# Moving a residual stage beside a recurrence, and reordering the maxima of an attention loop

## The chip, the cores and the metric

The kernel runs on one core of one Trainium2 chip. The metric is the device time of one execution in microseconds (us); the time of a kernel is the median of several runs. The engines are named as in the profile: PE is TensorE (PEld its weight loads), DVE is VectorE, ACT is ScalarE, POOL is GpSimd, SP is SyncE, which here only issues DMAs.

## The reference

The input `x` has 2 batches of 2048 positions with 256 features. A recurrent layer comes first, then mixture-of-experts attention, each with a layer norm ahead and a residual behind:

```python
x = x + rnn(layernorm(x), Wi, bi, Wh, bh)       # h = tanh(Wi x_t + bi + Wh h + bh)
x = x + ffn(layernorm(x), Wq, Wk, Ws, Wd, Wv, Wo)
# ffn: 8 heads of 64, 5 experts, 2 of them chosen
q = (x @ Wq).reshape(b, t, h, dh).transpose(0, 2, 1, 3)
k = (x @ Wk).reshape(b, t, h, dh).transpose(0, 2, 1, 3)
gl_v = (x @ Ws).reshape(b, t, h, e)
wv = _topk_mask(gl_v, SEL) * jax.nn.sigmoid(gl_v)
xv = jnp.einsum('btd,edk->btek', x, Wv)
v = jnp.einsum('bthe,btek->bhtk', wv, xv)
scores = jnp.einsum('bhid,bhjd->bhij', q * scale, k)
probs = jax.nn.softmax(scores, axis=-1)
attn = jnp.einsum('bhij,bhjd->bihd', probs, v)
mask_o = _topk_mask((x @ Wd).reshape(b, t, h, e), SEL)
out = jnp.einsum('bthe,bthk,ekd->btd', mask_o, attn, Wo)
```

Everything is float32.

## The kernel before, in words

**Layout.** Position `n * 16 + s` belongs to segment `n` (128 of them, on the partitions) and to chunk `s` (16 of them). A chunk is thus one step of all 128 segments, and the recurrence over 2048 positions is run on 128 segments side by side.

**Preparation** (L219 to L246). Groups of 1, 1, 2, 4, 4, 4 chunks: statistics on DVE (`stats`, L122 and L123), an inverse root from a bit trick (`guess`, L129 to L135) and four Newton steps of three tiny DVE operations each (`newton`, L142 to L146); normalisation on POOL (L156), four PE transposes (L231), a copy on ACT (L235), the input projection on PE, and ACT adds the sum of the two biases (`bsum`) on the way to `xi` (L246).

**Recurrence** (L261 to L294). `run("a")` starts every segment from zero and takes 16 steps; its last states become the start states `ends` of the segments behind. `run("b")` takes the 16 steps again from these and keeps every state in `hs`. A step is 16 weight loads and products (L283), four additions on DVE (L290) and four tanh on ACT (L293). Then DVE compares the last states of the two runs (L300 to L305), PE sums the verdict over the partitions (`pc`, L307), DVE makes it a flag (`again`, L309), and every engine loads it and branches (L310, L311). If the states still differ, the run is repeated under the branch; with these inputs it isn't.

**Residual stage** (L319 to L384), in two halves of 8 chunks. PE turns the states back (`tpb`, L334), DVE adds them to `x` (L335), SP stores the sum (`x1d`), DVE makes statistics and scales of batch 0. POOL and DVE normalise one chunk of each pair, PE turns it (`tpc`, L349), ACT copies it to `xn2T` (L352); PE makes the gate logits (`pg`, L359), ACT copies them to `gates_all` (L367). For each of the 16 chunks PE makes the experts' values (`pxv`, L372), ACT or DVE copies them (L381, L383) and SP stores them (`xvd`, L384). Batch 1 does this later, inside attention (`load_late` to `logits_late`).

**Attention** (from L497). A unit is one (batch, head) and one block of 512 queries; there are 64. A unit has 8 tiles of scores, `c` = 0 to 7, each for 256 keys (128x1024); a step `T` makes two, so four steps make a unit, and the boundary step is `T % 4 == 0`. The life of a tile:

- `scores`: PE writes it to one of two PSUM buffers (`s`, L503); `stage`: ACT copies it to SBUF (`p`, L514); `largest`: DVE takes the running elementwise maximum (`m`, L525; in the last tile `mh`, `m`, `mm`, L528 to L531). Tile 0 has no `m`; the `m` of tile 1 reads the copy of tile 0.
- In the next unit's boundary step PE turns the maximum (`pm`, L538), DVE reduces it (`mq`, L543), and PE spreads it over the partitions (`pt`, L553), which ACT copies to `top` (L556).
- From five steps behind on, `subtract` takes the maximum from the tile (L563; DVE for tiles 0 and 1, POOL for the rest), `exponential` is on ACT (L566), `products` on PE (`o`, L576), `fold` adds tiles in pairs with a DMA issued from POOL's queue (L588), `sums` makes the denominators on PE (`d`, L597).
- The closing of a unit: `take`, `take_sums` (`os`, L612 to L620), `close`: PE turns it (`po`, L629), DVE makes `den`, its reciprocal, `mr` and `pro` (L631 to L642), and `gather` adds it to memory (L684).

Keys (`pk`), queries (`pq`), the experts of batch 1 (`pv`, L463) and the value mixes (`fetch`, `xq`, `v`) of a head are made inside the loop. `gates` ranks the experts of half the chunks (`choose`, L160 to L195: ACT copies the logits and a ramp, DVE compares, POOL counts). Everything small in PSUM (`pm`, `pt`, `po`, `pk`, `pq`, `pv`, `py`, `pz`, `mh`, `wp`) comes from one pool of two buffers, `misc`.

**What sets the order.** Up to attention a scheduler orders each engine's instructions. Attention is in an order written out by hand, and each engine does its queue in it. A step lists: `take`; the subtraction of tile 0 where the step is the one in which a unit's subtractions begin (`T % 4 == 1`); one exponential; for each new tile scores, stage, largest; the subtractions and the fold; the list `before` of this step; products and sums; the other exponential; the list `behind` of this step. The lists are filled ahead by `at(table, T, f, ...)`:

```python
for t in new:
    ss = scores(t)
    stage(t, ss)
    largest(t, ss)
...
    at(before, T1, turn_max, u)
    at(before, T1, reduce_max, u)
    at(behind, T1, spread_max, u)
```

Since `close` of an earlier unit comes into the list `behind` of the same boundary step ahead of `spread_max`, PE has `po` before `pt`. Where two engines read the same scores in PSUM, one waits for the other: `m` of a tile waits for its copy.

Of the kernel before, what the change touches and what calls it, by code (L numbers as in the profile page):

```python
# [14 lines left out]
P = 128  # L15
# [5 lines left out]
def rnn_then_switchhead_kernel(  # L21
# [60 lines left out]
    nc.vector.tensor_tensor(bsum, bias[:, 0, :], bias[:, 1, :], ALU.add)  # L82
# [67 lines left out]
    def scales(pool, mv, n, nm):  # L150

        neg, v, y = guess(pool, mv, n, nm)
        return neg, newton(pool, v, y, n, range(4), nm)
# [6 lines left out]
    def choose(pool, b, c0, n, half, nm, logits):  # L160
# [8 lines left out]
        nc.scalar.copy(  # L169
# [3 lines left out]
        if not half:  # L173
            sg = pool.tile([P, n, HE], F32, tag="sg", bufs=1, name=f"sg{nm}")
            nc.scalar.activation(sg, gl, AF.Tanh, scale=0.5)
        later = []
        for d in range(1, E):
            a = pool.tile([P, n, H, E - d], F32, tag=f"later{d}", bufs=1, name=f"lt{nm}_{d}")
            nc.vector.tensor_tensor(a, g0[:, :, :, d:E], g[:, :, :, 0 : E - d], ALU.is_gt)
            later.append(a)  # L180
# [19 lines left out]
    NS = P  # L200

# [7 lines left out]
    nc.vector.memset(ends, 0.0)  # L209
    nc.vector.memset(ones, 1.0)  # L210

    with tc.tile_pool(name="prep", bufs=3) as pp, tc.tile_pool(
# [3 lines left out]
    ) as ps_t:  # L216
        c0 = 0
        for n in (1, 1, 2, 4, 4, 4):
            mv = pp.tile([P, n * B, 2], F32, tag=f"mv{n}", name=f"mva{c0}")  # L219
            for c in range(c0, c0 + n):  # L220
                for b in range(B):
                    stats(lnp, mv[:, (c - c0) * B + b, :], xt[c][:, b, :], f"a{c}_{b}")
            neg, y = scales(lnp, mv, n * B, f"a{c0}")
            for c in range(c0, c0 + n):
                xn = pp.tile([P, B, D], F32, tag="xn", name=f"xn{c}")
                for b in range(B):
                    normalize(xn[:, b, :], xt[c][:, b, :], neg, y, (c - c0) * B + b)
                tp = ps_t.tile([P, KC, B, P], F32, tag="tp", name=f"tpa{c}")
                for kc in range(KC):
                    for b in range(B):  # L230
                        nc.tensor.transpose(  # L231
                            tp[:, kc, b, :], xn[:, b, kc * P : (kc + 1) * P], ident
                        )
                xnT = pp.tile([P, KC, B, P], F32, tag="xnT", name=f"xnT{c}")
                nc.scalar.copy(xnT, tp)  # L235
                for mc in range(KC):
                    px = ps_xi.tile([P, B, P], F32, tag="px", name=f"px{c}_{mc}")
                    for kc in range(KC):
                        nc.tensor.matmul(
                            px.rearrange("p b n -> p (b n)"),  # L240
                            lhsT=wi[:, kc, mc * P : (mc + 1) * P],
                            rhs=xnT[:, kc].rearrange("p b n -> p (b n)"),
                            start=kc == 0,
                            stop=kc == KC - 1,
                        )
                    nc.scalar.activation(  # L246
                        xi[:, mc, c], px, AF.Identity, bias=bsum[:, mc : mc + 1]
                    )
            c0 += n

# [6 lines left out]
    with tc.tile_pool(name="step", bufs=3) as sp, tc.tile_pool(  # L257
        name="ps_h", bufs=1, space=PSUM
    ) as ps_h, tc.tile_pool(name="ps_c", bufs=1, space=PSUM) as ps_c:

        def run(nm, from_zero, keep_states):  # L261
            prev = None if from_zero else (lambda kc, b: ends[:, kc, b, 0:NS])
            for s in range(S):
                dst = {}
                if keep_states:
                    h = hs[:, :, s]
                elif s == S - 1:
                    h = ends[:, :, :, 1:]
                else:
                    h = sp.tile([P, KC, B, NS], F32, tag="h", name=f"h{nm}_{s}")  # L270
                for b in range(B):
                    if prev is None:
                        for mc in range(KC):
                            nc.scalar.activation(h[:, mc, b, :], xi[:, mc, s, b, :], AF.Tanh)
                        continue
                    ph = [
                        ps_h.tile([P, NS], F32, tag=f"ph{b}_{mc}", name=f"ph{nm}_{s}_{b}_{mc}")
                        for mc in range(KC)
                    ]
                    pre = sp.tile([P, KC, NS], F32, tag=f"pre{b}", name=f"pre{nm}_{s}_{b}")  # L280
                    for mc in range(KC):
                        for kc in range(KC):
                            nc.tensor.matmul(  # L283
                                ph[mc],
                                lhsT=wh[:, kc, mc * P : (mc + 1) * P],
                                rhs=prev(kc, b),
                                start=kc == 0,
                                stop=kc == KC - 1,
                            )
                        nc.vector.tensor_tensor(  # L290
                            pre[:, mc, :], ph[mc], xi[:, mc, s, b, :], ALU.add
                        )
                        nc.scalar.activation(h[:, mc, b, :], pre[:, mc, :], AF.Tanh)  # L293
                prev = lambda kc, b, h=h: h[:, kc, b, :]  # L294

        run("a", True, False)
        run("b", False, True)
        N = KC * B * NS
        off = sp.tile([P, KC, B, NS], F32, tag="off", bufs=1, name="off")
        nc.vector.tensor_tensor(off, hs[:, :, S - 1], ends[:, :, :, 1:], ALU.subtract)  # L300
        good = sp.tile([P, KC, B, NS], F32, tag="good", bufs=1, name="good")
        nc.vector.tensor_scalar(good, off, TOL, None, ALU.is_le)
        nc.vector.scalar_tensor_tensor(good, off, -TOL, good, ALU.is_ge, ALU.mult)
        count = sp.tile([P, 1], F32, tag="count", bufs=1, name="count")
        nc.vector.tensor_reduce(count, good.rearrange("p c b n -> p (c b n)"), AX.X, ALU.add)  # L305
        pc = ps_c.tile([1, 1], F32, tag="pc", name="pc")
        nc.tensor.matmul(pc, lhsT=count, rhs=ones, start=True, stop=True)  # L307
        again = sp.tile([1, 1], I32, tag="again", bufs=1, name="again")
        nc.vector.tensor_scalar(again, pc, float(P * N) - 0.5, None, ALU.is_lt)  # L309
        flag = nc.values_load(again[0:1, 0:1], min_val=0, max_val=1)  # L310
        with tc.If(flag > 0):  # L311
            with tc.For_i(0, NS - 2, 1):
                nc.vector.tensor_copy(ends[:, :, :, 1:], hs[:, :, S - 1])
                run("c", False, True)

    with tc.tile_pool(name="rnn", bufs=2) as rp, tc.tile_pool(  # L319
        name="ln", bufs=2  # L320
    ) as lnp, tc.tile_pool(name="ps_tb", bufs=2, space=PSUM) as ps_t, tc.tile_pool(
        name="ps_tc", bufs=2, space=PSUM
    ) as ps_c, tc.tile_pool(name="ps_g", bufs=2, space=PSUM) as ps_g, tc.tile_pool(
        name="ps_x", bufs=2, space=PSUM
    ) as ps_x:
        GC = NCH // 2
        for g in range(2):
            mv = rp.tile([P, GC, 2], F32, tag="mv", name=f"mvb{g}")
            for k in range(GC):
                c = g * GC + k  # L330
                tp = ps_t.tile([P, B, KC, P], F32, tag="tp", name=f"tpb{c}")
                for b in range(B):
                    for kc in range(KC):
                        nc.tensor.transpose(tp[:, b, kc, :], hs[:, kc, c, b, :], ident)  # L334
                nc.vector.tensor_tensor(  # L335
                    xt[c], xt[c], tp.rearrange("p b c d -> p b (c d)"), ALU.add
                )
                nc.sync.dma_start(out=x1d[c], in_=xt[c])
                stats(lnp, mv[:, k, :], xt[c][:, 0, :], f"b{c}")
            neg, y = scales(lnp, mv, GC, f"b{g}")  # L340
            for k in range(0, GC, 2):
                c = g * GC + k
                xn = rp.tile([P, 2, D], F32, tag="xn2", name=f"xn2_{c}")
                tp = ps_c.tile([P, KC, 2, P], F32, tag="tc", name=f"tpc{c}")
                for o in range(2):
                    eng = nc.vector if o else nc.gpsimd
                    normalize(xn[:, o, :], xt[c + o][:, 0, :], neg, y, k + o, eng)
                    for kc in range(KC):
# [168 lines left out]
    def largest(t, ss):  # L517
        u, c = t // HC, t % HC
        if c == 0:
            return  # L520
# [430 lines left out]
```

## Time and profile before

| what | us |
|---|---|
| median of 3 runs (lowest, highest) | 1719.53 (1718.27, 1722.62) |
| the profiled execution | 1725.14 |
| its span | 1723.4 |
| preparation, until the recurrence starts | 57.2 |
| both runs of the recurrence, last product of PE | 112.8 |
| the flag `again` made | 116.4 |
| PE's first work behind the branch | 121.6 |
| PE's first work of attention (`pq`) | 174.2 |
| `pt` of the first unit, of the second | 209.9, 239.0 |
| a unit of attention in steady parts | 21.0, 21.0, 20.9, 23.2 in turn |

The page has the busy time of each engine first, then rows in which each digit is the busy share of a fortieth of the span (43 us). A group line gives the line of the code, engine, operation, the tile written and those read, then after the bar the total and mean duration, and the idle time ahead of it with what ended it. A line of the timeline has start, duration, and in brackets the idle time before it. A line of waits has the waiting instruction, the one it waited for, and the total in us, the number of times and the longest.

### The profile page before, as it was taken

Reading aid. Unit: us, or ns where it says so; the run is one execution under the profiler, and the core shown is the slowest. Engines: PE = TensorE matmul, PEld = TensorE weight load, DVE = VectorE, ACT = ScalarE, POOL = GpSimd, SP = SyncE. Lnnn points to the kernel's source line nnn. Section 1 sums busy time; section 2 is a strip of 40 time slices with the busy share of each in tenths; the row PEclk is TensorE's granted clock in tenths of the full one; section 3 lists DMA queues with packets and bytes.
Section 4 is the critical chain, followed back from the end, with each engine's and each line's share of the span. In section 5 each row is a group of like instructions: output and inputs, shape, how many; then the busy total and the mean of one; then the engine's idle time right before and its main releaser. Section 6 shows DMA issues by size and latency. Waiting matters only on the chain.

```text
span 1723.4 us, 27125 instructions
## 1 busy us (share of the span) xinstructions
PE 1571.2 (91%) x10338; PEld 623.2 (36%) x10338; DVE 1312.7 (76%) x1861; ACT 1229.2 (71%) x1609; POOL 1264.5 (73%) x832
## 2 busy tenths in 40 slices
PE   6978689999989999999999999999999999999986
PEld 5976223232223333333323343333333333333234
DVE  5464588989887876678887668888888888888752
ACT  3642468787777887678887667787878787878861
POOL 3001667888778987679998757888888888888870
PEclk9998889999999999999999999999999999999999
DMA  4003157788777877678887656788888888888752
GB/s 152 1 34 116 54 132 175 174 181 171 153 155 159 165 159 162 153 154 161 166 174 161 153 133 164 167 160 169 162 170 161 169 162 169 162 168 182 150 121 80
DMA packets 88918, 254.74 MB, mean 148 GB/s; under 512 B 12176, under 2 KB 33488, under 8 KB 88784
## 3 DMA queue, kind: packets, MB, share of 16 engines
q0 software_dynamic: 43200, 163.60, 52.0%
q1 hardware_dynamic: 43952, 88.76, 16.1%
q8 instruction: 83, 1.36, 0.3%
q10 hardware_dynamic: 1632, 0.61, 0.1%
q14 instruction: 51, 0.42, 0.1%
HBM read 62.08 MB, written 50.33 MB: 65 GB/s over the span
## 4 chain that ended last, share of the span: by engine, by line
PE 49%; DVE 23%; ACT 11%; issue 5%; DMA 4%; POOL 1%; SPq 0%; ACTq 0%; DVEq 0%; POOLq 0%
PE s L503 20%; PE o L576 13%; DVE m L525 11%; ACT p L514 7%; PE d L597 4%; PE pq L443 3%; DVE p L563 3%; PE pt L553 2%; PE pk L424 2%; DVE mq L543 2%; DVE xq L488 2%; ACT p L566 2%; DVE v L494 1%; DMA p<-p 1%; PE pz L715 1%
## 5 line engine op out<-in xcount | busy, mean ns | idle before, releaser
L563 POOL TENSOR_TENSOR p<-p,top 128x1024 f32<-128x1024 f32 x381 | 1049.4, 2996 | 19.7 <-ACT top L556 19.7
L566 ACT ACTIVATE p<-p 128x1024 f32<-128x1024 f32 x512 | 540.0, 1066 | 79.2 <-DVE p L563 77.2
L503 PE MATMUL s<-qs,k 64*128 64x512 f32 x1024 | 525.9, 632 | 18.7 <-DVE m L525 18.4
L503 PE MATMUL s<-q,k 64*128 64x512 f32 x1024 | 526.1, 632 | 10.8 <-DVE m L525 10.1
L514 ACT COPY p<-s 128x1024 f32<-128x1024 f32 x512 | 494.4, 1015 | 20.7 <-PE s L503 17.4
L576 PE MATMUL o<-p,v 128*32 128x512 f32 x4096 | 493.1, 598 | 10.8 <-DVE os L613 7.5
L525 DVE TENSOR_TENSOR m<-s,m 128x1024 f32<-128x1024 f32 x320 | 391.8, 1224 | 136.5 <-ACT p L514 119.4
L588 POOL DMA_DIRECT2D p<-p x252 | 320.1, 1270 | 82.5 <-ACT p L514 35.5
L503 PEld LDWEIGHTS s<-qs,k 64*128 64x128 f32 x1024 | 173.0, 189 | 162.4 <-DVE m L525 86.3
L576 PEld LDWEIGHTS o<-p,v 128*32 128x32 f32 x4096 | 112.7, 109 | 315.6 <-issue 191.0
L503 PEld LDWEIGHTS s<-q,k 64*128 64x128 f32 x1024 | 172.9, 189 | 148.4 <-DVE m L525 70.1
L563 DVE TENSOR_TENSOR p<-p,pt 128x1024 f32<-128x1024 f32 x131 | 158.5, 1210 | 0.1
L525 DVE TENSOR_TENSOR m<-s,p 128x1024 f32<-128x1024 f32 x64 | 78.4, 1224 | 83.9 <-ACT p L514 83.5
L597 PE MATMUL d<-p,ones 128*32 128x512 f32 x1040 | 136.2, 592 | 0.7 <-DMA p<-p 0.7
L684 POOL DMA_DIRECT2D yd<-pro x48 | 42.3, 882 | 123.6 <-DVE pro L642 121.7
L556 ACT COPY top<-pt 128x512 f32<-128x512 f32 x64 | 37.5, 586 | 107.8 <-PE pt L553 107.8
L488 DVE TENSOR_TENSOR xq<-xq,wp 128x1280 f32<-128x1280 f32 x64 | 95.1, 1487 | 10.0 <-DMA xq<-xvd 8.0
L642 DVE TENSOR_TENSOR pro<-po,mr 128x1280 f32<-128x1280 f32 (+1 forms) x67 | 95.9, 1431 | 2.7
L494 DVE TENSOR_REDUCE v<-xq 128x256 f32<-128x1280 f32 x64 | 94.5, 1476 | 0.1
L156 POOL TENSOR_SCALAR xn<-x,mb,zb 128x256 f32<-128x256 f32 x8 | 5.2, 656 | 107.8 <-DVE zb L146 90.9
L553 PE MATMUL pt<-ident,mq 128*128 128x128 f32 x256 | 42.3, 289 | 43.1 <-DVE mq L543 42.4
L443 PE MATMUL pq<-xn2T,wq 128*32 128x512 f32 x512 | 61.6, 598 | 5.7 <-DVE xq L488 4.6
(139 smaller groups left out, 1544.7 us busy)
## 6 DMA issues: line engine op xcount, KB each, us to landing
p<-p POOLq DMA_DIRECT2D x252, 512.0 KB, 5.7
xq<-xvd SPq DMA_DIRECT2D x64, 640.0 KB, 6.2
yd<-pro POOLq DMA_DIRECT2D x48, 640.0 KB, 6.8
qs<-q SPq DMA_DIRECT2D x64, 128.0 KB, 2.3
yd<-pro SPq DMA_DIRECT2D x8, 640.0 KB, 3.8
y<-yd SPq DMA_DIRECT2D x8, 640.0 KB, 6.1
x<-in_x SPq DMA_DIRECT2D x16, 256.0 KB, 5.5
x1d<-x SPq DMA_DIRECT2D x16, 256.0 KB, 2.0
```

The lines of the kernel that those rows point to most:

```text
L443: nc.tensor.matmul(pq[at_col : at_col + 32, :], lhsT=wq[:, kc, h * DH + g : h * DH + g + 32], rhs=xn2T[:, kc, b, n * QB : (n + 1) * QB], s ...
L488: nc.vector.tensor_tensor(xq, xq, wp.unsqueeze(2).to_broadcast([P, 4, DH, E]), ALU.mult)
L494: nc.vector.tensor_reduce(v_of[i][:, 4 * part : 4 * part + 4, :], xq, AX.X, ALU.add)
L503: nc.tensor.matmul(ss[:, o, :], lhsT=k_of[i][half, c, :], rhs=q_of[i, n][o][half, :], start=True, stop=True,)
L514: nc.scalar.copy(p, ss)
L525: nc.vector.tensor_tensor(m, ss, ring[t - 1] if c == 1 else m, ALU.max)
L563: eng.tensor_tensor(p, p, top.unsqueeze(1).to_broadcast([P, 2, QB]), ALU.subtract)
L566: nc.scalar.activation(ring[t], ring[t], AF.Exp)
L576: nc.tensor.matmul(o_of[u][at_col : at_col + 32, :], lhsT=v_of[i][:, 2 * c + o, g : g + 32], rhs=ring[t][:, o, :], start=c == 0, stop=c == ...
L588: nc.gpsimd.dma_start(out=ring[t], in_=ring.pop(t + 1), accum_op=ALU.add)
L597: nc.tensor.matmul(den_of[u][32 * g : 32 * (g + 1), :], lhsT=ones32, rhs=ring[(t, t1)[g // 2]][:, g % 2, :], start=first, stop=last, tile_ ...
L642: nc.vector.tensor_tensor(dst, po[:, s : s + n, 0:DH].unsqueeze(2).to_broadcast([P, n, E, DH]), mr[:, s : s + n].unsqueeze(3).to_broadcast ...
```

## The change

1. **Preparation** is in a fixed order: `measure` (statistics and scales of a group), `turn_in` (normalise, transpose, copy) and `project_in`, with the turn of chunk c+1 ahead of the projection of chunk c. Groups are 1, 1, 2, 3, 4, 5. The addition of the biases moves behind the first group, two memsets go from DVE to POOL, and all Newton roots take three steps instead of four, the late ones too.
2. **The second run** carries, behind each of its steps `s`, work of the residual stage (`beside`): the turn of chunk s-1 on PE, its copy out of PSUM on ACT, the addition to `x` on POOL and the store from SP's queue; the statistics of chunk s-2 on DVE; from step 10 to 13 the roots of the first half; in the last two steps POOL's normalisation of chunks 0 to 7, two at a time. The transposes of these four pairs stand on PE ahead of `pc`. The branch that repeats the run also repeats all this, with `x` loaded anew.
3. **Behind the branch** come chunk 15, the second half's statistics, roots, normalisation and transposes, the gate logits, and the experts of the first four chunks only.
4. **The experts of chunks 4 to 15** of batch 0 go to the list `behind` of attention's steps 0 to 3, three a step; their SBUF buffer `xw` gets two copies.
5. **Gates**: the copy of the ramp goes from ACT to POOL, `sg` and three of the four `later` tiles get two buffers.
6. **Attention's steps** list both tiles' scores first, then the copies and maxima in another order: in a step that isn't a boundary the maximum of the second tile stands ahead of its copy and of the first tile's maximum; in the boundary step `turn_max` and `reduce_max` stand ahead of the maximum of tile 1. Tile 6 closes the running maximum instead of tile 7. `spread_max` comes first of what stands behind the products, so that PE has `pt` before `po`.

The core of the diff (the whole of the second run's new functions is in the words above):

```diff
@@ preparation @@
-        return neg, newton(pool, v, y, n, range(4), nm)
+        return neg, newton(pool, v, y, n, range(3), nm)
...
+        for n in (1, 1, 2, 3, 4, 5):
+            groups.append((c0, n))
+            c0 += n
...
+        measure(*groups.pop(0))
+        nc.vector.tensor_tensor(bsum, bias[:, 0, :], bias[:, 1, :], ALU.add)
+        for c in range(NCH):
+            while groups and groups[0][0] <= c + 2:
+                measure(*groups.pop(0))
+            if c == 0:
+                turn_in(0)
+            if c + 1 < NCH:
+                turn_in(c + 1)
+            project_in(c)
@@ second run @@
+    def turn_back(c, nm, eng=None):
+        tp = pst.tile([P, B, KC, P], F32, tag="tp", name=f"tpb{nm}{c}")
+        for b in range(B):
+            for kc in range(KC):
+                nc.tensor.transpose(tp[:, b, kc, :], hs[:, kc, c, b, :], ident)
...
+            hv = sp.tile([P, B, D], F32, tag="hv", bufs=2, name=f"hv{nm}{c}")
+            nc.scalar.copy(hv, tp)
+            nc.gpsimd.tensor_tensor(xt[c], xt[c], hv, ALU.add)
+        nc.sync.dma_start(out=x1d[c], in_=xt[c])
...
+    def beside(s):
+        if s >= 1:
+            turn_back(s - 1, "b")
+        if s >= 2:
+            stats_back(s - 2, "b")
+        part = s - GC - 2
+        if 0 <= part <= NEWTON:
+            roots(0, part, "b")
+        if s > GC + 2 + NEWTON or s == S - 1:
+            for c in range(2 * (s - GC - 3 - NEWTON), GC if s == S - 1 else 2 * (s - GC - 2 - NEWTON), 2):
+                xn_of[c] = norm_back(c, "b", pool2)
...
+            run("b", False, True, ps_h, beside)
...
+            for c in range(0, GC, 2):
+                turn_norm(c, xn_of.pop(c), "b")
+            pc = ps_c.tile([1, 1], F32, tag="pc", name="pc")
@@ behind the branch @@
+        for c in range(EARLY, S):
+            if c == S - 1:
+                turn_back(c, "d", nc.vector)
+            stats_back(c, "d")
+        for part in range(NEWTON + 1):
+            roots(1, part, "d")
+        for c in range(0, GC, 4):
+            logits(c)
+        for c in range(GC, S, 2):
+            xn_of[c] = norm_back(c, "d", (nc.vector, nc.gpsimd))
+        for c in range(4):
+            first_experts(c)
+        for c in range(GC, S, 2):
+            turn_norm(c, xn_of.pop(c), "d")
+        for c in range(GC, S, 4):
+            logits(c)
@@ gates, late roots, experts @@
-        nc.scalar.copy(
+        nc.gpsimd.tensor_copy(
             rank.rearrange("p c h e -> p (c h) e"),
...
-        xw = ap.tile([P, DH, E], F32, tag="xw", bufs=1, name=f"xw{b}_{c}")
+        xw = ap.tile([P, DH, E], F32, tag="xw", bufs=2, name=f"xw{b}_{c}")
...
+            for c in range(4, NCH):
+                at(behind, (c - 4) // 3, experts, b, c)
@@ attention @@
-        if c < HC - 1:
+        if c != HC - 2:
...
-        at(before, T1, turn_max, u)
-        at(before, T1, reduce_max, u)
-        at(behind, T1, spread_max, u)
+        at(first_behind, T1, spread_max, u)
...
+            fresh = sub and sub[0] % HC == 0
...
-            for t in new:
-                ss = scores(t)
-                stage(t, ss)
-                largest(t, ss)
-            if sub and sub[0] % HC:
+            ss = [scores(t) for t in new]
+            if new:
+                stage(new[0], ss[0])
+            if T % U_T == 0:
+                if new:
+                    stage(new[1], ss[1])
+                if 0 < T <= NT:
+                    turn_max(T // U_T - 1)
+                    reduce_max(T // U_T - 1)
+                if new:
+                    largest(new[1], ss[1])
+            elif new:
+                largest(new[1], ss[1])
+                stage(new[1], ss[1])
+            if fresh:
+                subtract(sub[1])
+            if T % U_T and new:
+                largest(new[0], ss[0])
+            if sub and not fresh:
                 subtract(sub[0])
...
-            for f in behind.pop(T, []):
+            for f in first_behind.pop(T, []) + behind.pop(T, []):
                 f()
```

## The prediction

> **What bounds the kernel now.** First the page: TensorE is busy 91% of the span, no other engine over 76%. It dips in the slices at 86 to 215 us (43 us each).
>
> ```profile
> span 1723.4 us, 27125 instructions
> PE 1571.2 (91%) x10338; PEld 623.2 (36%) x10338; DVE 1312.7 (76%) x1861; ACT 1229.2 (71%) x1609; POOL 1264.5 (73%) x832
> PE   6978689999989999999999999999999999999986
> POOL 3001667888778987679998757888888888888870
> ```
>
> Then the busy time by stretches of the front (PE, PEld, DVE, ACT, POOL, clock, DMA share, GB/s), and one of steady attention.
>
> ```profile
> 100.00:110.00 10.00, 10.00 (x92) 10.00 (x92) 6.59 (x23) 6.92 (x23) 0.00 (x0) 1.00 0.01 2
> 130.00:140.00 10.00, 5.03 (x33) 3.25 (x31) 10.00 (x43) 0.00 (x0) 0.98 (x2) 0.92 0.58 213
> 140.00:150.00 10.00, 9.75 (x48) 8.76 (x47) 5.50 (x25) 2.67 (x5) 2.82 (x5) 0.56 0.14 52
> 200.00:220.00 20.00, 11.57 (x30) 4.71 (x32) 16.75 (x22) 7.95 (x11) 16.95 (x21) 0.67 0.19 66
> 1360.00:1444.00 84.00, 80.41 (x554) 25.80 (x550) 71.76 (x81) 68.77 (x79) 73.81 (x44) 1.00 0.82 165
> ```
>
> The recurrence is bound by TensorE's weight loads, with VectorE and ScalarE at two thirds and GpSimd idle. The residual stage is bound by VectorE. Attention is TensorE with 4% idle. The timelines show two places: TensorE comes back 5.0 us after the flag, and ScalarE stands still for GpSimd's gates in the first attention steps.
>
> ```profile
> 116.41 0.15 DVE L309 TENSOR_SCALAR again<-pc 1x1 int32<-1x1 f32 x1 [0.28 <-PE pc L307]
> 121.55 3.65 PE L334 MATMUL tpb<-ident,hs 128*128 128x128 f32 x16 [5.18 <-PEq L311]
> 192.07 0.46 ACT L169 COPY rank<-ramp 128x320 f32<-128x320 f32 x1 [4.49 <-POOL gates_all L195]
> ```
>
> Then the waits from 262 to 1660 us (total, times, longest) and one hand-over between units.
>
> ```profile
> PE pt L553 <- DVE mq L543: 39.3, 49, 2.2
> PE s L503 <- DVE m L525: 10.8, 28, 0.6
> DVE m L525 <- ACT p L514: 182.9, 137, 2.9
> ```
>
> ```profile
> 1418.05 0.69 PE L503 MATMUL s<-qs,k 64*128 64x512 f32 x1
> ...
> 1422.41 0.66 PE L629 MATMUL po<-ident,os 128*128 128x128 f32 x4
> 1423.71 0.65 PE L553 MATMUL pt<-ident,mq 128*128 128x128 f32 x4 [0.65 <-DVE mq L543]
> ...
> 1423.57 0.15 DVE L631 TENSOR_REDUCE den<-po 128x4 f32<-128x8 f32 x1
> ...
> 1424.20 1.49 DVE L642 TENSOR_TENSOR pro<-po,mr 128x1280 f32<-128x1280 f32 x1
> 1425.61 1.21 DVE L563 TENSOR_TENSOR p<-p,pt 128x1024 f32<-128x1024 f32 x1
> 1426.88 2.55 DVE L525 TENSOR_TENSOR m<-s,m 128x1024 f32<-128x1024 f32 x2
> ```
>
> Each unit loses 0.65 us at `pt`: the spread maximum waits for `mq`, which VectorE reaches after an `m` that waited for ScalarE's copy.
>
> **What the Trainium skill says.** "PSUM — Partial Sum Buffer", bank collisions: two engines may not be on one bank at once, readers included, so such accesses are ordered by semaphores. The trace agrees: `m` waits 182.9 us for copies that only read the same scores; the change turns some of these orders round. Same page, engine vs sequencer instructions: matmuls start in program order. Agrees: behind `pt` stand scores whose inputs are ready. "TensorE: Matmul & The Clock Gate", Part 1: an idle window of about 3.4 us halves the clock. Agrees: 0.56 in 140:150, where 16 gate matmuls take 3.71 us against 1.92 warm. "SBUF — State Buffer", who interferes with whom: VectorE operations with two SBUF inputs block GpSimd's reads. Agrees in direction: the 128x1024 subtraction takes 2.33 us in the quiet stretch at 211.5, 2.996 in the mean.
>
> **The change, part by part.**
>
> *Preparation.* GpSimd's first normalisation starts at 12.16; 16 tiny VectorE operations at 0.20 us (4 of the guess, 12 of Newton) lead to it and `bsum` (needing the bias DMA) stands ahead. One Newton step less is 3 x 0.20 = 0.6; the rest of about 4 us is start-up, of which groups of 1, 1, 2, 3, 4, 5 keep about half. Taken: -2 (from 0 to -3.7).
>
> *Second run.* Fifteen residual chunks move beside steps of 1.79 us (16 weight loads of 0.112). TensorE gets 4 transposes a step, 0.54 warm: +8.1. ScalarE gets a 128x512 copy of 0.59 (0.692 x 1.79 + 0.59 = 1.83 of 2.33), VectorE statistics of 0.5 (1.18 + 0.5 = 1.7), both covered. GpSimd's 128x512 addition isn't in the trace; half the 128x1024 subtraction gives 1.17 to 1.5, covered too; SP's store waits for nothing on TensorE. If the cover fails, ScalarE's tanh chain lengthens: +8 to +12.
>
> *Flag.* TensorE's `pc` comes in order behind four pairs of normalised chunks, whose six last normalisations GpSimd starts after the addition of chunk 14: 1.3 + 6 x 0.6 = 4.9, then four transposes and `pc`, so about 7.0 after the run against 3.7: +3.3 (0 to +5). It is followed by the same 5.0.
>
> So TensorE resumes at about 131.5 against 121.5: -2 + 8.1 + 3.3, and 0.5 for its cold restart.
>
> *Flag to attention.* From 52.7 us (121.5 to the first `pq` at 174.2) to: chunk 15 and its statistics, cold, 0.9; 16 gate matmuls cold 3.7, 16 warmer 2 to 3; the second set of roots runs beside these on VectorE (13 x 0.2 = 2.6); four experts 4 x 1.2 = 4.8; four turns 2.4; gates 3.8; sum 18.8 (17 to 23, if `xw`'s stores, 1.9 each in the trace, hold experts up). Attention starts at 150.3: -24.
>
> *First steps of attention.* Twelve experts of 1.08 come back, three a step: 13 us of TensorE and 12 x 0.45 of ScalarE (its 128x320 copies). Their cover is the idle at `s` behind ScalarE's rank copies (2.0 + 3.2 + 3.5 and 3.1 at `pt`, 184 to 210 us). The rank copy moves to GpSimd, so ScalarE no longer stands 4.49 there, but GpSimd still makes 7.2 + 5.9 + 7.2 + 5.9 us of gates before the first subtractions, and `pv` and `pm`/`pt` share two PSUM buffers. I take `pt` of unit 0 at 42 us after the start (35.7 before), of unit 1 at 69.5 (64.8): +4.7 (0 with full cover, +13 with none). Front at unit 1: -24 + 4.7 = -19.
>
> *Steady attention, gain.* With `m` of a tile ahead of its copy, and `mq` ahead of the `m` of chunk 1, `mq` ends some 3.3 us after a boundary step starts; `pt` is reached at 1.92 + 0.58 + 1.85 = 4.4. The 0.65 goes. In a head's four units (TensorE's own work 20.35, 18.55, 22.15, 20.35 us with 1, 0, 2, 1 key or query blocks of 1.8) the idle now is 0.65, 1.87, 1.05, 0.65.
>
> *Steady attention, loss.* `po` now stands behind `pt`, so `den` starts at 4.4 + 0.64 + 0.64 = 5.7; it was 1423.57 - 1418.05 = 5.5. VectorE's chain is thus no earlier, while TensorE is 0.65 earlier. VectorE then does, in its new order, three small operations and `pro` (to 7.8), the subtraction of chunk 0 (9.0), `m` of chunk 3 (10.15), whose copy on ScalarE, 1.01 behind, frees the buffer for chunk 4's scores at 11.2. TensorE is there after scores 1.92, products 1.85, sums 0.86 from 5.6, at 10.2: a wait of 1.05. Then subtraction and `m` of chunk 2 end at 12.52, 0.34 late for chunk 5. Loss 1.39 a unit (0 if VectorE is earlier; 2.2 if the subtraction or `pro` runs at the long end). Units become 20.35 + 1.39 = 21.74, 19.94, 23.54, 21.74: 21.74 on average, against 21.53 measured (21.0, 21.0, 20.9, 23.2): +0.2. Over the 27 undisturbed units 35 to 61 that is +6; in the eight units 14 to 17 and 30 to 33, late normalisation fills VectorE and I add +6; in 2 to 13 and 18 to 28 waits at `pt` above 0.65 go: -4. Sum +8. The third late Newton step less is 0.6 on VectorE, hidden.
>
> *Sum.* -19 - 0.5 + 8 = -11.5 (-0.5: the last units, without blocks). Span 1723.4 becomes 1711.9, its execution 1725.1 becomes 1713.6. That execution is 5.6 above the median of the runs, 1719.5, so the median I forecast is **1708**.
>
> **Rivals.**
>
> *Cover for the new order.* The 1.39 is half hidden, since other work on TensorE (turns, output projections) stands ahead of chunk 4's scores in many units, and `pro` and the subtraction take their short ends; 0.7 x 46 units = -32 more: 1676. For it: VectorE is busy 72 of 84 us, so it has slack. Against: the order on it is fixed, and `pro` can't start before `po`.
>
> *Slower: the VectorE chain behind `pro`.* One mechanism: with `po` behind `pt`, `pro` - subtraction - `m` - copy holds chunk 4's scores by 2.1 instead of 1.39 a unit, at +0.7 x 46 = +32: 1740. It decides from 11.5/46 = 0.25 us a unit beyond my estimate, 1.64. For it: VectorE and GpSimd contend, and two-input operations on the path could be longer.
>
> *Front given back.* The first two units are bound by GpSimd's gates and subtractions (16.95 of 20 us busy at 200:220), so the earlier start is mostly waited for: +12 there: 1720.
>
> *The change does not do what it says.* The redo under the flag costs nothing unless taken, and the run before shows that it isn't; with the fixed order, the moves are in the code. No weight.
>
> **Numbers.** Likeliest 0.50 (own range 1698 to 1718), cover 0.20 (1668 to 1690), slower chain 0.20 (1728 to 1752), front given back 0.10 (1715 to 1726). I call 0.3%, 5.2 us, the least that a measurement of this kernel can tell from none. Faster (below 1714.4): 0.42 + 0.20 = 0.62; within: 0.08 + 0.07 + 0.01 = 0.16; slower: 0.22, mostly the chain. The range 1670 to 1735 leaves out most of the slower case's upper part and a little below.
>
> **What would show it.** Attention's first `pq` near 150; 15 residual chunks inside the second run at 2.33 us a step; `again` some 7 us behind it; no wait of `pt` for `mq`; a new wait of `s` for ScalarE's copy of about 1 us a unit. Wrong if `s` waits over 1.64 a unit, or not at all, or if unit 1's `pt` isn't 19 us earlier.

## The result and the profile after

The changed kernel takes 1708.09 us (median of 4 runs, 1706.6 to 1710.59), against 1719.84 before: ratio 0.993, 95% interval 0.9918 to 0.9942. Its profiled execution took 1710.59, 2.5 above that median; the execution of before was 5.3 above its own, so the spans differ by 14.6 where the medians differ by 11.8. Readings of one trace can thus be some 3 us off in their sum. The lines that answer to those shown of before, first the page:

```profile
span 1708.8 us, 27047 instructions
...
PE 1572.1 (92%) x10338; PEld 621.9 (36%) x10338; DVE 1307.3 (77%) x1805; ACT 1242.4 (73%) x1624; POOL 1287.0 (75%) x861
...
PE   6988799999989999999999999999999999999986
```

Stretches, columns as before:

```profile
100.00:110.00 10.00, 9.55 (x86) 9.31 (x85) 8.66 (x35) 6.45 (x21) 5.35 (x5) 1.00 0.31 116
...
130.00:140.00 10.00, 8.36 (x36) 7.97 (x37) 5.09 (x20) 0.85 (x2) 2.85 (x6) 0.50 0.08 28
...
200.00:220.00 20.00, 10.63 (x51) 2.84 (x49) 18.11 (x17) 8.98 (x11) 12.87 (x8) 0.80 0.40 109
...
1346.00:1430.00 84.00, 80.30 (x549) 25.53 (x548) 71.25 (x81) 67.55 (x78) 72.83 (x44) 1.00 0.82 161
```

At 100:110 DVE and POOL now work beside a PE that is almost full. At 130:140, behind the branch, PE's granted clock is half (0.50). Steady attention is as full as before (80.30 against 80.41 of 84). PE's return after the flag and the first attention work, in the timeline:

```profile
123.74 0.14 DVE L400 TENSOR_SCALAR again<-pc 1x1 int32<-1x1 f32 x1 [3.28 <-PE pc L398]
...
128.64 0.87 PE L328 MATMUL tpbd<-ident,hs 128*128 128x128 f32 x3 [4.93 <-PEq L402]
...
150.40 1.49 PE L524 MATMUL pq<-xn2T,wq 128*32 128x512 f32 x11
```

PE's and DVE's waits from 262 to 1660, then one hand-over between units:

```profile
PE s L584 <- ACT p L595: 44.9, 57, 1.5
PE pt L633 <- DVE mq L623: 9.0, 11, 2.7
```

```profile
DVE m L605 <- PE s L584: 86.4, 106, 2.8
DVE m L605 <- ACT p L595: 38.1, 50, 1.5
```

```profile
1409.27 0.65 PE L633 MATMUL pt<-ident,mq 128*128 128x128 f32 x4
1409.76 0.60 PE L709 MATMUL po<-ident,os 128*128 128x128 f32 x4
...
1415.92 0.69 PE L584 MATMUL s<-qs,k 64*128 64x512 f32 x1 [0.93 <-ACT p L595]
```

`pt` no longer waits 39.3 but 9.0; a new wait of `s` for ACT's copy, 44.9, has taken its place. `m` waits 38.1 for copies instead of 182.9, and 86.4 for the scores themselves.

The stages in the two traces (times of PE), beside the terms on record. Attention's start is the first `pq` behind the last gate logits; in the changed kernel two products of `pq` already stand among the turns at 144.86.

| term | before | after | measured | on record |
|---|---|---|---|---|
| recurrence starts | 57.17 | 52.71 | -4.5 | -2 |
| both runs, to the last product or turn of PE | 55.66 | 63.64 | +8.0 | +8.1 |
| from there to PE's return behind the branch | 8.72 | 12.29 | +3.6 | +3.3 |
| return to attention | 52.67 | 21.76 | -30.9 | -33.9, and 0.5 for cold |
| attention starts | 174.22 | 150.40 | -23.8 | -24 |
| from there to `pt` of unit 1 | 64.81 | 76.69 | +11.9 | +4.7 |
| `pt` of unit 1 to 35 | 819.4 | 815.1 | -4.3 | +2 |
| `pt` of unit 35 to 62 | 579.3 | 580.7 | +1.4 | +6 |
| from there to the end | 85.7 | 86.0 | +0.3 | -0.5 |

The measured terms sum to -14.5, the difference of the spans; -11.5 was on record. That the total came so close is in good part luck. Ahead of attention two errors of 2.5 cancel, a preparation that gained more than forecast and a way to attention that gained less. Behind it two larger ones nearly cancel: the first units cost 7 more than forecast, the rest 10 less.

### The profile page after: what moved, and what is told of

It is laid out like the page before. It is cut to its first block, busy times and chain, and to the rows that moved or that the text cites. A ratio compares the mean times of both kernels' runs of the same rounds, so it can differ in the third digit from the quotient of the medians.

```text
span 1708.8 us, 27047 instructions
## 1 busy us (share of the span) xinstructions
PE 1572.1 (92%) x10338; PEld 621.9 (36%) x10338; DVE 1307.3 (77%) x1805; ACT 1242.4 (73%) x1624; POOL 1287.0 (75%) x861
## 4 chain that ended last, share of the span: by engine, by line
PE 50%; DVE 17%; ACT 9%; issue 9%; DMA 4%; POOL 0%; SPq 0%; ACTq 0%; DVEq 0%; POOLq 0%
PE s L584 20%; PE o L656 13%; DVE m L605 8%; ACT p L595 7%; PE d L677 3%; PE pq L524 3%; PE pk L505 3%; DVE p L643 3%; PE pz L795 2%; DMA p<-p 2%; PE pv L544 2%; ACT p L646 1%; DVE v L575 1%; DMA xq<-xvd 1%; PE po L709 1%
## 5 line engine op out<-in xcount | busy, mean ns | idle before, releaser
L595 ACT COPY p<-s 128x1024 f32<-128x1024 f32 x512 | 511.2, 1011 | 264.1 <-DVE m L605 140.8
L668 POOL DMA_DIRECT2D p<-p x252 | 301.2, 1195 | 84.2 <-PE o L656 32.6
L584 PEld LDWEIGHTS s<-qs,k 64*128 64x128 f32 x1024 | 168.7, 188 | 182.7 <-ACT p L595 81.1
L584 PEld LDWEIGHTS s<-q,k 64*128 64x128 f32 x1024 | 168.6, 188 | 168.0 <-ACT p L595 64.4
L677 PE MATMUL d<-p,ones 128*32 128x512 f32 x1040 | 143.9, 593 | 2.2 <-DMA p<-p 2.1
L569 DVE TENSOR_TENSOR xq<-xq,wp 128x1280 f32<-128x1280 f32 x64 | 95.1, 1486 | 13.8 <-DMA xq<-xvd 11.8
L677 PEld LDWEIGHTS d<-p,ones 128*32 128x32 f32 x1040 | 35.2, 110 | 87.4 <-issue 77.6
L623 DVE TENSOR_REDUCE mq<-pm 128x4 f32<-128x512 f32 x64 | 44.3, 692 | 25.1 <-PE pm L618 23.5
L505 PE MATMUL pk<-xn2T,wk 128*32 128x512 f32 x512 | 62.4, 598 | 0.0
```

What stands on the lines that cost most here:

```text
L505: nc.tensor.matmul(pk[at_col : at_col + 32], lhsT=wk[:, kc, h * DH + g : h * DH + g + 32], rhs=xc[:, kc, c0 // 2 : (c0 + HC) // 2, o, :], ...
L584: nc.tensor.matmul(ss[:, o, :], lhsT=k_of[i][half, c, :], rhs=q_of[i, n][o][half, :], start=True, stop=True,)
L595: nc.scalar.copy(p, ss)
L668: nc.gpsimd.dma_start(out=ring[t], in_=ring.pop(t + 1), accum_op=ALU.add)
L677: nc.tensor.matmul(den_of[u][32 * g : 32 * (g + 1), :], lhsT=ones32, rhs=ring[(t, t1)[g // 2]][:, g % 2, :], start=first, stop=last, tile_ ...
```

## Experiments

All ratios are to the kernel before, with 95% intervals.

**Front alone and order alone.** Two kernels separate the diff: `front_only` is the changed kernel with the old attention loop, `order_only` the kernel before with the new one.

> The changed kernel with the old order of attention's steps (tile by tile scores, copy, maximum; turn_max behind the maxima; spread_max behind close; the maximum closed by tile 7). Theory A, from the two traces: the gain is made before attention's second unit (-11.9 there), and the reorder nets only about -3 (-4.8 from the second unit to the last, +2.1 in the tail). Then this kernel takes 1710 to 1713, units go back to 21.0, 21.0, 20.9, 23.2 and pt waits 0.65 for mq. Rival, the account on record: the front gives -19 at the second unit and the reorder costs +8. Then it takes 1698 to 1702. Second rival: the first steps' stalls at s (6.3 and 3.1 for a copy behind a maximum) come from the new order; then the second unit's pt stands at 215 to 222 instead of 227 and the time is 1703 to 1707.

> The kernel before with the new order of attention's steps, all else as before. Theory A: about -3, so 1715 to 1719 (steady units 21.45, 20.4, 23.2, 21.45). Rival, the account on record: +8, so 1726 to 1730. Second rival (the first steps' stalls come from the order): the second unit's pt goes from 239 to 245 or later, and the time to 1722 to 1726.

Measured: front alone 1707.93 (0.9915, 0.99 to 0.9929); order alone 1720.59 (0.9992, 0.9982 to 1.0001). The front is the whole gain. The order alone is worth -3.1 to +0.2 us by its interval, and with the front the medians differ by 0.2; so +8 is ruled out, and -3 lies at the edge of what fits. Unit 1's `pt` stands at 225.6 with the old order, 227.1 with the new: the first steps' stalls aren't the order's. PE's waits with the old order, from 262 to 1645:

```profile
PE pt L634 <- DVE mq L624: 38.5, 48, 1.8
PE s L584 <- DVE m L606: 10.8, 28, 0.6
```

The 39 at `pt` and the 45 at `s` are exchanged for each other.

**po first.** The second question was what in the new order eats its gain.

```diff
-        at(first_behind, T1, spread_max, u)
+        at(behind, T1, spread_max, u)
```

> The changed kernel with one edit: spread_max stands behind close again, so that PE has po before pt in the boundary step. Account on record: po behind pt makes den late and this feeds the chain pro, subtraction, maximum, copy that holds chunk 4's scores; with po first den starts 0.5 earlier, the wait of s falls from 0.95 to 0.45 in some 50 units, and the time falls by 20 to 25, to 1683 to 1688. Theory A, from the trace after: den starts at once behind the maximum of tile 1 on DVE (1409.26 + 1.15 = 1410.41), which itself waits 0.77 for ScalarE's copies; po ends at 1410.36, at the same moment, so an earlier po changes nothing: 1706 to 1711, and a wait of s as before.

Measured: 1691.38 (0.9818, 0.9803 to 0.9832), 17 faster than the change. Both expectations fall. The wait of `s` is still 42.7 in 262:1627, so `po` behind `pt` is not its main cause (only in one steady unit of four does it fall, from 0.94 to 0.50); yet the time falls. It does so in units 10 to 35: `pt` of unit 9 stands at 400.4 against 400.7, of unit 35 at 1025.8 against 1042.2. These are the units with late normalisation, batch 1's experts and output projections. Of the 16.4 gained between the first scores of units 10 and 36, 13.7 lie in twelve of them, 16 to 23 and 32 to 35. In their boundary steps the list `behind` also holds `pgl` (logits), `pv` (experts), or `pz` and `py` (output projections), all ahead of `close`. So the edit moves `pt` behind these too: PE's order in unit 33 is `pt`, `pz`, `py`, `po` in the changed kernel, and `pz`, `py`, `po`, `pt` here. PE's waits between units 10 and 35 in the changed kernel,

```profile
PE pt L633 <- DVE mq L623: 7.3, 5, 2.7
PE pgl L837 <- ACT xw L552: 3.3, 6, 0.6
PE po L709 <- ACT gates_all L844: 2.9, 8, 0.4
PE po L709 <- ACT yT L786: 2.7, 4, 0.7
...
PE py L779 <- DVE z L802: 2.1, 4, 0.5
```

and with `po` first:

```profile
PE po L709 <- DVE os L700: 4.7, 3, 2.0
...
PE po L709 <- DVE z L802: 1.3, 4, 0.8
PE pgl L837 <- ACT xw L552: 1.1, 2, 0.6
```

A wait of `po` for `yT` or `gates_all` is no wait for data: those copies read what `py` or `pgl` left in the small PSUM buffer that `po` takes next (`pgl` and `tpl` come from the pool `misc` as well). In the twelve units PE's idle time falls from 16.3 to 4.6, and waits for such readers are 9 of it. The 7.3 at `pt` for `mq` lie in other units, and 4.7 at `po` for `os` takes their place there.

**Two tests of the small buffers.** `pt_freed` lets DVE's two subtractions read `top` in SBUF, so that `pt`'s buffer is free early:

```diff
-        eng, top = (nc.vector, top_of[u][0]) if c < 2 or last else (nc.gpsimd, top_of[u][1])
+        eng, top = (nc.vector, top_of[u][1]) if c < 2 or last else (nc.gpsimd, top_of[u][1])
```

> The changed kernel with one edit: DVE's subtractions of tiles 0 and 1 take the maximum from its copy in SBUF (top) instead of from PSUM (pt), so that pt's small PSUM buffer is free when ACT has copied it, about 5 earlier. Theory D for the 17 that po first gained (all in the units 10 to 35): with pt first, pt holds one of the two small buffers until the second subtraction, and py, pz, po, pgl and tpl take turns in the other. Then this kernel gains most of it in the same units, 1692 to 1700, if the subtraction from SBUF is not slower. Rival: the gain comes from po's place alone (den and pro earlier in these units); then nothing is gained here, 1706 to 1712, or up to 1725 if DVE and POOL get into each other's way.

Measured: 2180.77 (1.2666, 1.2647 to 1.2686). It says nothing on the buffers, since the subtraction itself became more than three times as long. The group in the changed kernel and here, and two of its instructions in the timeline, with POOL's beside them:

```profile
L643 DVE TENSOR_TENSOR p<-p,pt 128x1024 f32<-128x1024 f32 x131 | 158.3, 1209 | 0.2
...
L643 DVE TENSOR_TENSOR p<-p,top 128x1024 f32<-128x1024 f32 x131 | 530.5, 4050 | 0.0
```

```profile
1420.31 1.22 DVE L643 TENSOR_TENSOR p<-p,top 128x1024 f32<-128x1024 f32 x1
...
1422.57 7.97 DVE L643 TENSOR_TENSOR p<-p,top 128x1024 f32<-128x1024 f32 x1
...
1421.26 2.69 POOL L643 TENSOR_TENSOR p<-p,top 128x1024 f32<-128x1024 f32 x1
...
1424.31 5.13 POOL L643 TENSOR_TENSOR p<-p,top 128x1024 f32<-128x1024 f32 x2
```

The first, begun ahead of POOL's, takes 1.22; the second, begun while POOL (from 1421.26) works through three subtractions, ends 1.1 behind the last of them (1429.44). The Trainium skill, "SBUF — State Buffer", "Who interferes with whom", says that a DVE instruction with two SBUF inputs contends with a GpSimd instruction that reads SBUF, over ports that are an exclusive lock. The trace agrees, and here the hold lasted through three instructions of POOL in a row.

`pt_po` goes the other way: `close` comes directly behind `pt`, ahead of the rest of the list.

```diff
-        at(behind, T1 + LAG + 2, close, u)
+        at(second_behind, T1 + LAG + 2, close, u)
...
-            for f in first_behind.pop(T, []) + behind.pop(T, []):
+            for f in first_behind.pop(T, []) + second_behind.pop(T, []) + behind.pop(T, []):
```

> The changed kernel with one edit: in the boundary step close (po and pro) comes right behind pt, ahead of everything else in the list behind (output projections, late turns and logits). Theory D, the two small PSUM buffers: pt holds one until DVE's second subtraction and po the other until pro has read it, about 2.4 behind po, so in the units 10 to 35 what comes behind (pz, py, tpl, pgl) waits for pro each time; steady units as in the changed kernel. Time 1712 to 1735. Rival: what po first gained was the earlier den and pro alone; then an early po behind pt gains nearly the same, 1690 to 1696.

Measured: 1745.61 (1.0151, 1.0134 to 1.0168), beyond the expected range but on its side; an early `po` alone doesn't bring the gain. PE's new waits between units 10 and 35:

```profile
PE pz L795 <- DVE pro L722: 9.5, 4, 2.4
PE pgl L837 <- DVE pro L722: 9.2, 4, 2.3
PE pv L544 <- DVE pro L722: 9.2, 4, 2.3
```

`pt` has one buffer and `po` the other, and what comes next waits 2.3 for `pro`, about the 2.4 expected, once in each of the twelve units. Unit 35 stands at 1071.0 (1042.2 in the change), the steady units are unchanged (21.45). Of the 29 lost between units 10 and 35, 19 are more idle time of PE; the other 10 are slower work, since the granted clock there was 0.97 in the mean against 0.99. Five stretches at half clock, 31 us in all, each begin during one of these waits or within 1.3 us of its end.

The two runs together make the two small buffers the main cause: PE waits for their readers in just these units, fewer such waits make it faster, more make it slower. They don't show it as the only one. In units 16 to 19 a wait of `s` of 0.64 goes as well with `po` first (2.5 of the 16.4), which fits the rival of an earlier `den` and `pro`. A kernel with a third small buffer was not run.

**The chain at the fresh step.** The steady wait of `s` is 0.93 for ACT's copy of tile 3, which waits for `m` of tile 3. The next edits are in the step `T % 4 == 1`: in `copy_first` the copy goes ahead of its maximum; in `sub_last` the subtraction of tile 1 goes behind the maximum of tile 2; `both` has the two, `best` also `po` first.

```diff
# copy_first
+            elif new and fresh:
+                stage(new[1], ss[1])
+                largest(new[1], ss[1])
             elif new:
                 largest(new[1], ss[1])
# sub_last
-            if fresh:
-                subtract(sub[1])
             if T % U_T and new:
                 largest(new[0], ss[0])
+            if fresh:
+                subtract(sub[1])
```

> The changed kernel with one edit, in the step with T % 4 == 1: the copy of tile 3 stands ahead of its maximum, so that the copy waits only for PE and the maximum for the copy. Plain reading of the waits (s waits for ACT's copy, 44.9 in all, 0.98 in a steady unit): without that wait some 34 to 46 units gain 0.95 each, 1665 to 1676. Theory B, VectorE's chain is the cause and the copy only its last link: chunk 4's scores then start at once, but chunk 5's wait for the maximum of tile 2, which ends at the same moment as before (1417.04 in the unit after 1409.27), so 0.13 a unit at most: 1703 to 1709, and a wait of s for m of about 0.9 in its place.

> The changed kernel with one edit, in the step with T % 4 == 1: DVE's subtraction of tile 1 stands behind the maximum of tile 2 instead of ahead of it. Theory B: tile 2's maximum ends 1.13 earlier, but chunk 4's scores still wait 0.95 for the copy of tile 3, and chunk 5's come right behind: no gain, 1705 to 1710. Plain reading (VectorE's order doesn't matter where the wait is for ScalarE): the same. A rival in which the later subtraction delays the exponential and the products of tile 1: plus 0.25 a unit, 1715 to 1720.

> The changed kernel with both edits, the copy of tile 3 ahead of its maximum and the subtraction of tile 1 behind the maximum of tile 2. Theory B: neither edit gains alone and the two together gain 0.95 a unit less about 0.25 at the products of tile 1, whose exponential comes later, in the three of four units that wait: 0.7 x 3/4 x 46 = 24, so 1681 to 1688. Plain reading: the same as the copy alone.

> The two edits of the run before and in addition spread_max behind close (po before pt). Theory C, from the run with po first (-17, all of it in the units 10 to 35, where output projections and late normalisation share the two small PSUM buffers with pt; the steady units kept their wait of s of 0.98): the gains add up, 1691 - 24 = 1667, so 1663 to 1672. Rival: po first and the two edits shorten the same chain of VectorE, so that they overlap: 1676 to 1685.

Measured: copy first 1712.81 (0.9948, 0.9932 to 0.9965), subtraction last 1704.54 (0.9905, 0.9892 to 0.9918), both 1691.09 (0.982, 0.9805 to 0.9835), best 1682.37 (0.9778, 0.9761 to 0.9794). The copy first gains nothing (4.7 above the change); the wait only changes its name:

```profile
PE s L584 <- DVE m L605: 46.4, 50, 1.2
...
PE s L584 <- ACT p L595: 7.3, 13, 0.6
```

With both, from 262 to 1640, the wait of `s` falls from 44.9 to 9.4:

```profile
PE o L656 <- DVE os L693: 10.7, 15, 2.0
...
PE s L584 <- ACT p L595: 5.5, 13, 0.4
...
PE s L584 <- DVE m L605: 3.9, 6, 1.1
PE py L779 <- DVE p L643: 3.5, 4, 0.9
```

A steady unit of one block falls from 21.45 to 20.45 with both. The subtraction alone, of which no gain was expected, gives 0.32 (21.13), the share of chunk 5 that the prediction had as 0.34. Both gained 17, not 24, since units 24 to 35 lose 6 (unit 24's `pt` stands 6.8 ahead of the change's, unit 35's 0.5): there `pt` is held longer, until the later subtraction, for which `py` now waits 3.5. `best` keeps that wait (4.2) but loses those of `po` for `yT` and `gates_all`, and gains 9 over `both` and over `po` first. Since 17 and 17 make 26 and not 34, the gains overlap, as the rival of that expectation said. `best` is faster than the kernel before and the changed one.

**The front's terms.**

> The changed kernel with all 16 experts of batch 0 made ahead of attention, none in its first four steps. Account on record: twelve experts cost only 4.7 in the first two units, since they fill stalls, and would cost 12 x 1.2 = 14 plus waits for stores ahead: 1716 to 1720. Theory A: in attention they cost 11.9, by 13 of TensorE's work and by hand-overs of two PSUM buffers to ScalarE (2.1, 3.5, 1.0, 0.7, 0.5, 0.5 of waits); ahead of attention they cost 14 to 16: 1710 to 1713, with attention starting at 164 to 167 and the second unit's pt 65 later.

Measured: 1712.26 (0.994, 0.9926 to 0.9954). Attention starts at 164.29 instead of 150.40 and unit 1's `pt` comes 61.2 later instead of 76.7. The twelve experts cost 15.4 inside attention and 13.9 ahead of it: on balance no stall of the first steps covered them. Until unit 1's `pt` PE is busy 41.6 and idle 19.7 in this run, busy 56.8 and idle 19.9 in the changed kernel. PE's waits in this run from 164 to 226, and in the changed kernel from 150 to 228, show why (first this run's):

```profile
PE s L586 <- ACT p L597: 14.5, 6, 5.0
PE pt L635 <- DVE mq L625: 2.6, 1, 2.6
```

```profile
PE s L584 <- ACT p L595: 9.4, 2, 6.3
PE pv L544 <- DVE mm L611: 3.5, 1, 3.5
PE pv L544 <- ACT xw L552: 3.2, 3, 2.1
```

The experts do fill waits of the first steps (5.1 less at `s`, 1.8 less at `pt`), but they bring 8.4 of waits of their own (the lines of `pv`, two shorter ones for `q` and `k` with them), for the two small buffers. The 9.4 that is left at `s` stands behind the last of them, at 206.56 and 220.00.

`pc_ahead` puts `pc` ahead of the four turns:

```diff
-            for c in range(0, GC, 2):
-                turn_norm(c, xn_of.pop(c), "b")
             pc = ps_c.tile([1, 1], F32, tag="pc", name="pc")
             nc.tensor.matmul(pc, lhsT=count, rhs=ones, start=True, stop=True)
+            for c in range(0, GC, 2):
+                turn_norm(c, xn_of.pop(c), "b")
```

> The changed kernel with one edit: PE sums the verdict (pc) ahead of the four turns of normalised chunks, not behind them. If the flag's 3.3 (on record; measured 12.3 - 8.7 = 3.6 from the last product to PE's return) is the wait of the flag alone, PE returns at 125.3 instead of 128.6 and the time is 1704 to 1706. Theory F: PE itself must finish its turns at 123.5 before it can take the branch, so only the hand-over pc, again is saved, 0.4: 1706 to 1710, no difference that can be measured, though `again` is made near 121 instead of 123.7.

Measured: 1708.33 (0.9929, 0.9916 to 0.9942), no gain over the change, with the flag 3.2 earlier:

```profile
120.47 3.70 PE L361 MATMUL tpcb<-ident,xn2b 128*128 128x128 f32 x16
...
120.58 0.15 DVE L400 TENSOR_SCALAR again<-pc 1x1 int32<-1x1 f32 x1 [0.28 <-PE pc L396]
...
150.48 0.63 PE L524 MATMUL pq<-xn2T,wq 128*32 128x512 f32 x3
```

PE still turns until 124.2, and attention starts where it did (150.48 against 150.40). The 3.6 is PE's own queue, not the flag's lateness.

`prep_only` puts the new preparation, with four Newton steps, into the kernel before.

> The kernel before with the new preparation alone: fixed order, groups 1, 1, 2, 3, 4, 5, the biases' sum behind the first group, two memsets on POOL; Newton keeps its four steps. Account on record: -2 for the preparation, of which -0.6 is the third Newton step's absence, so -1.4: recurrence starts at 55.7, time 1718 to 1720. Theory E, from the DVE timelines: before, the scheduler put 11 statistics of other chunks between the first group's root steps (first normalisation at 12.16 against 8.42), so the order alone brings 4.5 less two roots of 0.2 x 3 on the way to the second chunk, about -3.5: recurrence at 53.5 to 54, time 1715 to 1718.

Measured: the recurrence starts at 54.90, 2.3 earlier; the time is 1721.21 (1.0002, 0.9992 to 1.0012), no difference. The order of the queue gives 2.3; by subtraction, the fourth Newton step's absence gives the other 2.2 of the 4.5. Why 2.3 at 55 us doesn't show in the time isn't settled: in the one trace attention starts 3.4 earlier (170.87), but the interval of the 14 runs reaches to -1.4 at best.

## Why the prediction was right, and where not

- **Run, flag, branch to attention:** right by their steps (+8.0, +3.6, -30.9). The flag's term has the right size, but `pc_ahead` shows that PE's own turns make it and not the wait for the flag. The last term lacks 3.0, most of it at chunk 15: from PE's return to the first gate product 3.3 passed, where 0.9 had been taken, and 2.13 of it is a stall for which the profile names no wait. The 32 gate products at half clock took 6.95, where 5.7 to 6.7 had been taken. The terms listed there make 17.6 to 18.6, a little less than the 18.8 stated.
- **The clock:** the half clock at 140:150 of before is in the trace, but an idle window of 3.4, which the forecast sets beside it, is not. Between PE's return and 138.5, where the half clock begins, its longest wait was 1.1; one of 1.94 was under way. In `pt_po` half clock comes with waits of 2.3.
- **Preparation:** the mechanism was right, the term mis-sized, -2 against -4.5. The step "3 x 0.20 = 0.6" counted one group, and the Newton step gave 2.2; the order gave 2.3, where 1.4 was left for it.
- **First steps of attention:** wrong in the step "their cover is the idle at `s`". In the two units PE's busy time grew by 13.8 and its idle time fell by only 1.9 (21.7 to 19.9): the stalls that the experts filled came back as 8.4 of waits at `pv` for the two small buffers. So +11.9, not +4.7. By the forecast's own last sign, unit 1's `pt` 19 earlier, it failed here: it was 11.9.
- **Steady gain:** right. The 0.65 at `pt` went in full.
- **Steady loss:** the chain was right, the size high: 1.39 a unit was forecast, and 21.45 less PE's own 20.35 is 1.10, of which 0.93 is the wait of chunk 4's scores. The mean unit is 21.61, not 21.74 (21.45, 20.36, 23.17, 21.45).
- **Units 10 to 35:** the step "late normalisation fills VectorE and I add +6" is wrong: the eight units it names took as long as before (0.3 less in the traces). What costs there are the two small PSUM buffers, and `pt` ahead of the other small work fills them: 17, measured by `po_first`. The rest of the new order gains as much: 1707.9 with the front and the old order, 1691.4 with the front and the new order but for `pt`. The order's gain was found and spent within the same diff.
- **Rivals:** "front given back" had the right place and, with 7 of its 12, part of the size, but not the cause. From attention's start to unit 1's `pt` 61.2 to 64.8 passed in the four kernels without the twelve experts there, whose attention starts between 164.3 and 174.2, and 73.9 to 77.4 in those with them; so it is the experts, not an earlier start that is waited for. The slower chain's 1.64 was not reached.

## What to carry to other kernels

Where many small operations share a pair of buffers, an operation that is moved forward also takes its buffer earlier and keeps it until its last reader is done. Ask what else needs a buffer in between. A wait's named partner is the last link of a chain: free it alone and the next link takes over, so look for the two edits that open both. A total that fits says little, until its terms are each set beside the trace.

## What had not been expected of the hardware

- A 128x1024 subtraction on DVE with both inputs in SBUF took 1.22 where it started ahead of POOL's and 7.97 where it started behind the first of three (mean of 131: 4.05); with the maximum in PSUM the mean is 1.21.
- Smaller operations of DVE were held as well. Beside POOL's 1.27 us additions in the second run of the changed kernel, a 128x8 operation took 1.20 instead of 0.17, until the addition had ended, and so did one at 109.80 (1.24). So was a third (128x512, at 118.11: 1.63, where before it took 0.69); no other DVE operation of that run with all its inputs in SBUF began inside one of these additions. The 39 additions of the recurrence that began inside one read PSUM, and took 0.28 to 0.29 as elsewhere. Behind each of the first two the recurrence waited 0.45 once. The lines of the first:

```profile
104.58 1.27 POOL L335 TENSOR_TENSOR x<-x,hvb 128x512 f32<-128x512 f32 x1 [0.95 <-ACT hvb L334]
...
104.68 1.20 DVE L134 TENSOR_SCALAR ybb<-ibb 128x8 int32<-128x8 int32 x1
...
106.47 2.05 PE L299 MATMUL phb<-hs,wh 128*128 128x128 f32 x16 [0.45 <-ACT hs L307]
```
